# A four-layer graph stack on one core: layer 1's pair rows turned round, its node updates set beside later pairs, the edge checks placed anew

## The chip, the core and the metric

The kernel runs on one core of one Trainium2 chip. It is one launch; the metric is the device time of that launch in microseconds. The core has five engines that run side by side and meet at semaphores: TensorE (PE in the profile; PEld are its weight loads), VectorE (DVE), ScalarE (ACT), GpSimd (POOL) and SyncE (SP), which here only starts transfers. Sixteen DMA engines move data between HBM and the on-chip memory SBUF; matrix products land in PSUM.

## The reference

Four graph layers follow each other on x (4096 nodes, 64 features) with one 4096 x 4096 matrix of edges of 0 and 1. Each layer takes h = relu(layernorm(x)) and adds its result to x. Layer 1 is the one that the change is about; layers 2 and 3 follow it.

```python
h = jnp.maximum(_layernorm(x, axis=-1), 0.0)
x = x + _L0_gnn_ref(h, adj, ...)          # attention of eight heads, then an output attention
# layer 1: c = 1 / r[0] ** 2
h = jnp.maximum(_layernorm(x, axis=-1), 0.0)
x_t = logmap0(h, c)
left, right = x_t @ w_att[:D, 0], x_t @ w_att[D:, 0]
adj_att = jax.nn.sigmoid(left[:, None] + right[None, :] + b_att[0]) * adj
x_local = logmap(h[:, None, :], h[None, :, :], c)          # for every pair of nodes
support_t = jnp.einsum('ij,ijd->id', adj_att, x_local)
x = x + proj(expmap(h, support_t, c), c)                   # node by node: roots, a tanh, divisions
# layer 2
h = jnp.maximum(_layernorm(x, axis=-1), 0.0)
deg = jnp.clip(jnp.sum(adj, axis=1, keepdims=True) + 1.0, 1.0, None)
z = jnp.concatenate([h, (adj @ h + h) / deg], axis=1) @ W + b
out = jax.nn.relu(z)
x = x + out / jnp.maximum(jnp.linalg.norm(out, axis=1, keepdims=True), 1e-12)
# layer 3: weights 0.5 ** (k - rank) for the last 100 edges of a row, by a running count of edges
h = jnp.maximum(_layernorm(x, axis=-1), 0.0)
x = x + w @ (h @ weight) + bias
```

## The kernel before, in words

The 4096 nodes are 32 blocks of 128 (NB = 32), or 8 groups of 512 (NG = 8). Node tiles such as `x` and `h` are 128 x 32 x 64. The program assumes that the edges are exactly 0 or 1 and checks this while it runs: the float matrix is read again in 64 pieces of 128 x 2048 (1 MB each), and `check_rows` (line 960) writes a count of odd values into a column of `bad`. If one is found, or if the inputs are out of range, a slower general program runs at the end. The list `todo` hands out the 64 pieces: `count_odd` (line 964) loads one and checks it, wherever it is called.

Stages, with their places in the profiled execution (microseconds from the start of the span):

**Layer 0**, up to about 1190. It is the larger part of the time, and the change does not touch it.

**The pairs of layer 1**, `pairs_fast`, 1193 to 1648. The distance and score of all node pairs are made group by group. A job is a pair of groups (gi, gj) with gj <= gi, so there are 36 jobs, eight of them on the diagonal. They run row by row with gi rising: (0,0), (1,0), (1,1), (2,0) and so on to (7,7). Jobs are pipelined by hand: while job n is summed (`turn`, `sums`, `last_column`), job n+1 is scored (`score_pair`, `factor`, `weigh`) and job n+2's distances are made (`distance`, `square`). Each job has four slots s = 0 to 3. All instructions of PE, DVE and ACT are issued in the written order (`in_order`); DMAs and GpSimd are not held to it. `bring` moves the sums of a finished job into VT (128 x 4096): line 2408 adds `accj` into the columns of gj, and on the diagonal lines 2406 and 2407 first set the columns of gi. `check_edges` checks one piece in slot 2 of each job and one more in slot 0 beside a diagonal job: 48 of the 64 pieces.

**The ends of layer 1**, `nodes`, built on `finish_steps` (line 2471 on) and `norm_steps`. A quarter is eight blocks (1024 nodes). For each quarter: PE folds VT into node rows (`pvt`, line 2471, evicted by line 2475), then DVE works down a chain of 46 instructions, 16 of them wide (128 x 260 to 128 x 512) and 30 on 128 x 8, with square roots (lines 2500, 2520 and, in the layernorm, 991) and a tanh (line 2503) on ACT. ACT loads another table of functions where root and tanh change places. The result is the new x, the new h, and h as a pair of float16 halves in `HH` (lines 2605 to 2612), which layer 2's matmuls read. The quarters run in rising order after the last pair, in `layers_fast`; at a wait in one quarter up to two steps of the next are put in.

**Layer 2**, `layers_fast`. For eight sets of four blocks (q = 0 to 7) `HH` times the edges (line 2754) and the counts of edges (`dc`, line 2764) are summed for the first half of the nodes; the edges come as bytes, 1 MB for each q (line 2749), in three buffers. Then pairs of groups go through `layer2_group` (first matmul `pz`, line 2680; last DVE step line 2723), while the second half's `segment` sums (lines 2802 and 2811) fill PE. `hT2` is h transposed, made group by group (lines 1008 and 1009).

**Layer 3**, the last loop of `layers_fast`. It has 64 iterations, each with four pairs of `ranks` matmuls (lines 2860 and 2868), `clamp` on DVE and ACT (lines 2884 and 2882), and four `sacc` matmuls of the iteration before (line 2892). Edges come in two transfers of 512 KB for every four iterations (line 2931). Two of every three iterations from the 17th on check half a piece (128 x 1024): 16 pieces in 32 halves; in those iterations three of the four clamps are on ACT. The pieces share two buffers, so a load starts when the piece before the last one is checked. This loop too is in the written order.

On GpSimd and its own queue stand, at the start of `layers_fast`, seven small loads of weights (lines 2566 to 2577), a scaling of one of them (line 2573) and several fills (lines 2579 to 2664).

Of the kernel before, what the change touches and what calls it, by code (L numbers as in the profile page):

```python
# [55 lines left out]
F_C = 1186.920286584489  # L56

HW = N // 2
NS = HW // G
HB = NB // 2  # L60
# [776 lines left out]
def kernel(  # L837
# [76 lines left out]
    bad = npool.tile([P, 2 * NB + 2 + NB // 2], F32, name="bad")  # L914
# [52 lines left out]
    todo = iter(range(2 * NB))  # L967
# [4 lines left out]
    def norm_steps(bs, wide, tag, act=True):  # L972
# [18 lines left out]
        nc.scalar.activation(var, var, AF.Sqrt, bias=eps_t, scale=1.0 / D)  # L991
        yield True
        nc.vector.reciprocal(var, var)
# [1259 lines left out]
    def pairs_fast(es, VT):  # L2253
# [16 lines left out]
        jobs = [(gi, gj) for gi in range(NG) for gj in range(gi + 1)]  # L2270
        edges, sig, far, accs, squares = {}, {}, {}, {}, {}

        with ExitStack() as ss:
# [129 lines left out]
            def bring(gi, gj):  # L2403
                if gi == gj:
                    acci = accs.pop(gi)
                    nc.vector.tensor_copy(VT[0:D, grp(gi)], acci[D : 2 * D])
                    nc.vector.tensor_copy(VT[D : 2 * D, grp(gi)], acci[0:D])
                nc.vector.tensor_tensor(VT[:, grp(gj)], VT[:, grp(gj)], accs.pop("j"), ALU.add)
                del far[gi, gj]
                for way in ways(gi, gj):  # L2410
                    del sig[way], edges[way]

            def check_edges():
                c = next(todo, None)
                if c is not None:
                    count_odd(work, c)
# [5 lines left out]
            with in_order():  # L2422
                for n in range(-2, len(jobs) + 1):
# [3 lines left out]
                    for s in range(4):  # L2427
# [11 lines left out]
                        if later:  # L2439
                            distance(*later, s)  # L2440
                            if s % 2:
                                square(*later, s - 1)
                        if s == 1 and soon:
                            factor(*soon)
                        if n >= 0 and (s == 2 or s == 0 and (not now or now[0] == now[1])):
                            check_edges()
# [5 lines left out]
    def finish_steps(bs, VQ, VT, fold_v, pabs, f, f2, kp, pf, ac2, wide, ps):  # L2452
# [14 lines left out]
        for g in range(bs.start // GB, bs.stop // GB):  # L2467
            pt = ps.tile([P, GB, D1], F32, name="pvt", tag="misc")
# [31 lines left out]
        nc.scalar.activation(un, un, AF.Sqrt)  # L2500
        yield True
        nc.vector.tensor_tensor(arg, un, kp[:, bs], ALU.mult)
        nc.scalar.activation(arg, arg, AF.Tanh)
        nc.vector.reciprocal(un, un)
# [7 lines left out]
        nc.vector.tensor_scalar(one2, xu, p2c, 1.0, ALU.mult, ALU.add)  # L2512
        nc.vector.tensor_tensor(den, ac2[:, bs], uu, ALU.mult)
# [6 lines left out]
        nc.scalar.activation(pp, pp, AF.Sqrt)  # L2520
# [5 lines left out]
        nc.vector.reciprocal(pp, pp)  # L2526
# [12 lines left out]
        yield from norm_steps(bs, wide, "fat")  # L2539
# [5 lines left out]
    def layers_fast(es, wide, *sums):  # L2545
        HO2 = N // 4
        NK = HO2 // G
        cp = es.enter_context(tc.tile_pool(name="lconst", bufs=1))
# [21 lines left out]
        for i, unit in enumerate((1.0 / VALH, 1.0 / (LO * VALH))):  # L2570
# [11 lines left out]
        HH, SS = (  # L2582
            t.rearrange("p (b s d) -> p b s d", s=2, d=D)
            for t in (XA_all.bitcast(F16)[:, 0:N], XA_all.bitcast(F16)[:, N:])
        )
# [10 lines left out]
        ready = []  # L2596

        QB = NB // 4  # L2600

        def nodes(bs):
            yield from finish_steps(bs, *sums, wide, ps)
            hs = wide.tile([P, QB, D], F32, name="hs", tag="fat")
            nc.scalar.activation(HH[:, bs, 0, :], h[:, bs], AF.Copy, scale=VALH)
            yield True
            ready.append(
                nc.vector.scalar_tensor_tensor(
                    hs, h[:, bs], VALH, HH[:, bs, 0, :], ALU.mult, ALU.subtract
                )  # L2610
            )
            nc.scalar.activation(HH[:, bs, 1, :], hs, AF.Copy, scale=LO)


        quarters = [nodes(slice(b, b + QB)) for b in range(0, NB, QB)]
        with in_order():
            for quarter, after in zip(quarters, quarters[1:] + [iter(())]):
                most = 7
                for wait in quarter:
                    for _ in range(min(2, most) if wait else 0):  # L2620
# [41 lines left out]

        hT2 = lp.tile([D + 1, N], F32, name="hT2")
        nc.gpsimd.memset(hT2[D : D + 1, :], 1.0)
        for b0 in range(0, NB, GB):
# [8 lines left out]
        def layer2_group(b0, part, deg):  # L2674
# [48 lines left out]
            nc.vector.tensor_tensor(lo, pu, SS[:, bs, 0, :], ALU.subtract)  # L2723
# [11 lines left out]
        def in_turn_all(*groups):  # L2735
            for pair in zip(groups[::2], groups[1::2]):
                in_turn(*pair)

# [5 lines left out]
        with tc.tile_pool(name="ps_nacc", bufs=6, space=PSUM) as ps_acc:  # L2744
            accs = [ps_acc.tile([P, G], F32, name="nacc", tag="nacc") for _ in range(NS)]
            dc = ps_acc.tile([P, G], F32, name="dc", tag="nacc")
            for q in range(NQ):
# [3 lines left out]
                for t in range(JT):  # L2751
                    j = q * JT + t
                    for k in range(NS):
# [4 lines left out]
                            start=(j == 0),  # L2758
                            stop=(j == NB - 1),
                        )  # L2760
                for t in range(JT):
                    j = q * JT + t
                    for k in range(NS):
# [4 lines left out]
                            start=(j == 0),  # L2768
                            stop=(j == NB - 1),
# [71 lines left out]
            for k in range(0, NS, 2):  # L2841
                in_turn(segment(k), segment(k + 1))
            rank_rows(pl, 1)
# [5 lines left out]
        c = next(todo)  # L2849
        rows = load_rows(work, c)  # L2850
        edges, accs, last, ready = None, {}, None, None
# [72 lines left out]
        with in_order():  # L2924
            for n in range(4 * PAIRS):
# [10 lines left out]
                checks = u and (n - PAIRS) % 3  # L2936
                w = clamp(pvs, checks)
                if checks:
                    if checks == 1:
                        check_rows(rows[:, 0 : HW // 2], c)  # L2940
                    else:
# [101 lines left out]
```

## Time and profile before

| what | value |
|---|---|
| median of three runs | 1974.12 us (1969.64 to 1977.29) |
| profiled execution, time | 1974.73 us |
| its span | 1973.0 us, mean granted TensorE clock 0.943 |
| PE, DVE, ACT, POOL busy over the span | 1773.5, 1596.4, 1424.0, 89.3 us |
| pairs of layer 1 | 1193 to 1648 |
| ends of layer 1 and the first half of layer 2's sums | 1648 to 1743 |
| groups of layer 2 | 1743 to 1812 |
| layer 3 | 1812 to 1966 |

The shares of busy time are means over stages with different limits, so the stages are read one by one. A row of the stage table gives a stretch, its length, then for PE, PEld, DVE, ACT and POOL the busy time and in brackets the count of instructions, then the granted clock of PE (1.00 is full), the busy share of the 16 DMA engines and the GB/s that they moved. In a timeline row the numbers are the start and the duration in us, and the bracket at the end is the idle time of that engine before it and what ended it. In a wait row they are the total, the count and the longest wait.

### The profile page before, as it was taken

The page shows a single profiled execution, that of the slowest core. Times are in us where ns is not written, and L with a number is a line of the kernel's source. Part 1 is how long each engine was busy: PE and PEld are TensorE (multiplying, and loading weights), DVE is VectorE, ACT ScalarE, POOL GpSimd, SP SyncE. Part 2 cuts the span into 40 slices and gives each one's busy share as a digit, 9 for nine tenths or more (in the row PEclk, how much of TensorE's full clock was granted, in tenths as well). Part 3 has the DMA queues.
Part 4 walks back from the last instruction along what each step waited for, and adds up shares of the span by engine and source line. Part 5 has one row for each costly group of instructions (what it writes and reads, how often), then busy time and mean ns, then how long its engine had stood idle before and what let it go on. Part 6 is the DMA issues. An engine that isn't in the chain of part 4 may idle for free. (4 is left out here: it accounts for less than half of the span.)

```text
span 1973.0 us, 44405 instructions
## 1 busy us (share of the span) xinstructions
PE 1773.5 (90%) x19367; PEld 827.7 (42%) x19367; DVE 1596.4 (81%) x2378; ACT 1424.0 (72%) x1461; POOL 89.3 (5%) x127
## 2 busy tenths in 40 slices
PE   5889999999999989998599968999999994899998
PEld 3444444454444445444244442233333332355433
DVE  5769998998779988997768867888887878755676
ACT  2769888899778887995579956777777772333565
POOL 2000100100000000000111100000000001000000
PEclk8889999999999999998699976999999996898999
DMA  8946665325211111102255515543443435342584
GB/s 112 178 127 103 103 102 71 143 107 199 114 50 50 50 50 55 56 2 76 87 182 182 191 34 193 171 144 118 150 144 122 139 103 194 129 128 88 165 276 158
DMA packets 136698, 239.06 MB, mean 121 GB/s; under 512 B 15607, under 2 KB 104999, under 8 KB 122759
## 3 DMA queue, kind: packets, MB, share of 16 engines
q1 hardware_dynamic: 121964, 194.00, 29.4%
q0 software_dynamic: 14528, 42.13, 12.3%
q8 instruction: 153, 2.51, 0.5%
q14 instruction: 53, 0.43, 0.1%
HBM read 245.37 MB, written 49.46 MB: 149 GB/s over the span
## 5 line engine op out<-in xcount | busy, mean ns | idle before, releaser
L1213 ACT ACTIVATE st<-srow,nt 128x2048 int8<-128x2048 f32 x352 | 682.9, 1994 | 90.3 <-DVE B L1219 89.0
L1219 DVE TENSOR_TENSOR B<-st,mres 128x1024 int32<-128x1024 int32 x256 | 311.6, 1220 | 65.1 <-PE accC L1549 39.4
L1549 PE MATMUL accB<-B,ybh 128*32 128x512 fp8e4 x3072 | 256.6, 383 | 18.7 <-DVE B L1219 18.5
L1549 PEld LDWEIGHTS <-ybh 128*32 128x32 bf16 (+1 forms) x6656 | 179.1, 97 | 210.9 <-issue 56.4
L1549 PE MATMUL accC<-B,ycn 128*32 128x512 fp8e4 x2272 | 227.8, 380 | 1.2 <-issue 1.2
L1549 PE MATMUL accC<-mres,ych 128*32 128x512 fp8e4 x2272 | 228.1, 381 | 0.0
L1549 PE MATMUL accD<-B,ybh 128*32 128x512 fp8e4 x2048 | 207.6, 384 | 2.1 <-DVE h L1681 2.1
L1207 DVE TENSOR_SCALAR st<-srow,nt 128x2048 uint8<-128x2048 f32 x160 | 205.3, 1284 | 1.8
L2363 PE MATMUL accj<-sg,who 128*64 128x512 f32 (+1 forms) x512 | 196.7, 614 | 6.4 <-DVE sg L2356 5.9
L2363 PE MATMUL acci<-sg,who 128*64 128x512 f32 (+1 forms) x512 | 196.7, 614 | 0.0
L2319 ACT ACTIVATE yt<-pu,consts 128x512 f32<-128x512 f32 x144 | 98.6, 686 | 97.9 <-PE pu L2318 97.8
L2308 ACT ACTIVATE sg<-pl,rb 128x512 f32<-128x512 f32 x256 | 160.7, 678 | 7.8 <-PE pl L2303 4.7
L1549 PEld LDWEIGHTS <-ych 128*32 128x32 f16 x4096 | 117.6, 97 | 115.3 <-issue 10.2
L1549 PE MATMUL accL<-B,ybh 128*32 128x512 fp8e4 x1536 | 158.0, 387 | 3.6 <-DVE h L1680 3.6
L960 DVE SCALAR_TENSOR_TENSOR raw<-raw 128x2048 f32<-128x2048 f32 (+1 forms) x80 | 148.4, 1856 | 3.3 <-DMA raw<-in_adj_dram 3.3
L1213 ACT ACTIVATE st<-srowo,nto 128x1024 int8<-128x1024 f32 x128 | 138.1, 1138 | 16.3 <-DVE B L1219 13.9
L1227 DVE TENSOR_TENSOR C<-B,mres 128x1024 int32<-128x1024 int32 x114 | 139.5, 1224 | 3.1
L1549 PE MATMUL accC<-C,ych 128*32 128x512 fp8e4 x1824 | 124.0, 383 | 5.3 <-DVE C L1227 5.2
L2882 ACT ACTIVATE w3b<-pv 128x512 int16<-128x512 f32 x160 | 85.3, 596 | 52.9 <-issue 34.3
L2356 DVE SCALAR_TENSOR_TENSOR sg<-pf,sg 128x512 f32<-128x512 f32 x112 | 72.1, 685 | 38.7 <-PE pf L2353 38.7
L2297 PE MATMUL pl<-nm,noid 128*128 128x512 fp8e4 x256 | 82.3, 393 | 13.7 <-ACT sg L2308 13.0
L1549 PEld LDWEIGHTS <-ycn 128*32 128x32 f16 x2272 | 66.1, 98 | 62.1 <-issue 3.2
(515 smaller groups left out, 2738.8 us busy)
## 6 DMA issues: line engine op xcount, KB each, us to landing
raw<-in_adj_dram SPq DMA_DIRECT2D x64, 1024.0 KB, 5.6
mo<-edges SPq DMA_DIRECT2D x32, 512.0 KB, 4.0
noedge<-nmo POOLq DMA_DIRECT2D x32, 512.0 KB, 3.9
nm<-noedge SPq DMA_DIRECT2D x64, 256.0 KB, 3.0
m<-edges SPq DMA_DIRECT2D x32, 512.0 KB, 5.5
srow<-srow_d SPq DMA_DIRECT2D x15, 1024.0 KB, 7.8
mres<-in_adj_dram POOLq DMA_DIRECT2D x8, 1024.0 KB, 36.1
edges<-in_adj_dram POOLq DMA_DIRECT2D x8, 1024.0 KB, 15.0
```

The source lines that it names most:

```text
L960: nc.vector.scalar_tensor_tensor(raw, raw, 0.0, raw, ALU.is_gt, ALU.not_equal, accum_out=bad[:, at : at + 1])
L1207: nc.vector.tensor_scalar(st[:, i, :].bitcast(U8), srow, negs[:, i : i + 1], EDGE, ALU.is_gt, ALU.mult)
L1213: nc.scalar.activation(st[:, i, :], srow, AF.Sign, bias=negs[:, i : i + 1], scale=-1.0)
L1219: nc.vector.tensor_tensor(B.bitcast(I32), st.bitcast(I32), edges.bitcast(I32), ALU.bitwise_and)
L1227: nc.vector.tensor_tensor(C.bitcast(I32), B.bitcast(I32), edges.bitcast(I32), ALU.bitwise_xor)
L1549: ins = nc.tensor.matmul(acc[k * O : (k + 1) * O, :], lhsT=values, rhs=moving(k), start=start, stop=stop,)
L2297: nc.tensor.matmul(pl, lhsT=noid, rhs=nm[:, b, :].bitcast(F8), start=True, stop=False)
L2308: nc.scalar.activation(sg[:, b0 + k, :], pl, AF.Sigmoid, bias=rb[:, j : j + 1], scale=1.0)
L2319: nc.scalar.activation(far[gi, gj][:, b, :], pu, AF.Sigmoid, bias=nb_t, scale=2.0 * DIST_K / (DIST_S * DIST_S),)
L2356: nc.vector.scalar_tensor_tensor(v[:, t, :], pf, F_K3, v[:, t, :], ALU.add, ALU.mult)
L2363: nc.tensor.matmul(acc[r : r + n, :], lhsT=XQ[:, src, cols], rhs=w, start=start, stop=stop)
L2882: nc.scalar.activation(wk, pvs[i, k], AF.Relu)
```

## The change

Five things are changed together.

1. `jobs` runs with gi falling: (7,0) to (7,7), then (6,0) and so on to (0,0). `bring` copies `accj` in row 7 and adds it elsewhere; the diagonal adds both halves of `acci`.
2. When an even row gi = 6, 4, 2 is done, `nodes(gi * GB, ...)` is put into the list `ends`: the quarter of groups gi and gi + 1. `end_nodes` takes one step of it in each of the four slots of a job (up to two near the end). Its PSUM tile comes from the pairs' `pf` pool. What is left after the last job, and the whole of quarter 0, run in `layers_fast` as before, up to three steps of quarter 0 at a wait.
3. In quarters that run beside pairs (`beside`), the three square roots are not ACT's but `inverse_root`: one DVE instruction on the bits, then three Newton rounds of four GpSimd instructions, all on 128 x 8.
4. Layer 2's first sums take q = 7 down to 0, and `hT2` is made from the last group down.
5. Checks: none in `pairs_fast` while `ends` is not empty; `some_checks` in layer 2; 29 pieces instead of 16 in layer 3, so that from the 7th iteration on each one checks half a piece. In the built program 27 pieces are checked beside pairs, 8 in layer 2 and 29 in layer 3.

In the built program quarter 1's last root stands on GpSimd's queue behind the loads and fills at the start of `layers_fast`.

```diff
+QB = NB // 4
+CHECKS_3 = 29
...
+    def inverse_root(name, v, pool):
+        y, t = (pool.tile([P, v.shape[1]], F32, name=n, tag=n) for n in (name, name + "t"))
+        nc.vector.tensor_scalar(
+            y.bitcast(I32), v.bitcast(I32), -0.5, ROOT_BITS, ALU.mult, ALU.add
+        )
+        for _ in range(3):
+            nc.gpsimd.tensor_tensor(t, y, y, ALU.mult)
+            nc.gpsimd.tensor_tensor(t, t, v, ALU.mult)
+            nc.gpsimd.tensor_scalar(t, t, -0.5, 1.5, ALU.mult, ALU.add)
+            nc.gpsimd.tensor_tensor(y, y, t, ALU.mult)
+        return y
...
-        nc.scalar.activation(var, var, AF.Sqrt, bias=eps_t, scale=1.0 / D)
-        yield True
-        nc.vector.reciprocal(var, var)
+        if beside:
+            nc.gpsimd.tensor_scalar(var, var, 1.0 / D, LN_EPS, ALU.mult, ALU.add)
+            yield True
+            var = inverse_root("ln_root", var, wide)
+            yield True
+        else:
...
-        jobs = [(gi, gj) for gi in range(NG) for gj in range(gi + 1)]
+        jobs = [(gi, gj) for gi in reversed(range(NG)) for gj in range(gi + 1)]
+        ends = []
...
+                accj = accs.pop("j")
+                if gi == NG - 1:
+                    nc.vector.tensor_copy(VT[:, grp(gj)], accj)
+                else:
+                    nc.vector.tensor_tensor(VT[:, grp(gj)], VT[:, grp(gj)], accj, ALU.add)
                 if gi == gj:
                     acci = accs.pop(gi)
-                    nc.vector.tensor_copy(VT[0:D, grp(gi)], acci[D : 2 * D])
-                    nc.vector.tensor_copy(VT[D : 2 * D, grp(gi)], acci[0:D])
-                nc.vector.tensor_tensor(VT[:, grp(gj)], VT[:, grp(gj)], accs.pop("j"), ALU.add)
+                    for to, r in ((0, D), (D, 0)):
+                        half = VT[to : to + D, grp(gi)]
+                        nc.vector.tensor_tensor(half, half, acci[r : r + D], ALU.add)
+                    if gi % 2 == 0 and gi:
+                        ends.append(nodes(gi * GB, lambda: ps_f.tile([P, G], F32, name="pf", tag="pf")))
...
+            def end_nodes(most):
+                while ends and most:
+                    wait = next(ends[0], None)
+                    if wait is None:
+                        ends.pop(0)
+                    most = 0 if wait else most - 1
...
+                        busy = bool(ends)
+                        if now:
+                            end_nodes(1 if later else 2)
                         if s == 1 and soon:
                             factor(*soon)
-                        if n >= 0 and (s == 2 or s == 0 and (not now or now[0] == now[1])):
+                        if n >= 0 and not busy and (s == 2 or s == 0 and (not now or now[0] == now[1])):
                             check_edges()
...
+        if beside:
+            yield False
+            norm, un = un, inverse_root("un_root", un, wide)
+            nc.gpsimd.tensor_tensor(norm, norm, un, ALU.mult)
+            nc.gpsimd.tensor_tensor(arg, norm, kp[:, bs], ALU.mult)
+            yield True
+            nc.scalar.activation(arg, arg, AF.Tanh)
...
-        nc.scalar.activation(pp, pp, AF.Sqrt)
+        if beside:
+            yield False
+            pp = inverse_root("pp_root", pp, wide)
...
-            for quarter, after in zip(quarters, quarters[1:] + [iter(())]):
-                most = 7
+            for quarter, after in zip(ends, ends[1:] + [iter(())]):
+                most = 12
                 for wait in quarter:
-                    for _ in range(min(2, most) if wait else 0):
+                    for _ in range(min(3, most) if wait else 0):
...
-        for b0 in range(0, NB, GB):
+        for b0 in reversed(range(0, NB, GB)):
...
+        def some_checks(left):
+            n = len(todo) - CHECKS_3
+            with tc.issue_after(valued[-1].ins):
+                for _ in range(-(-n // left)):
+                    count_odd(work, todo.pop(0))
...
-            for q in range(NQ):
+            for n, q in enumerate(reversed(range(NQ))):
...
-                checks = u and (n - PAIRS) % 3
+                checks = n >= 4 * PAIRS - 2 * CHECKS_3
```

`valued` holds the last DVE step of each layer 2 group, so that the checks there are issued after it.

## The prediction

> **What bounds the kernel now.** I read the stage table first, then PE's waits between the stages, then the timelines of DVE and GpSimd in that gap, last the loads of layer 3.
>
> ```profile
> 1193.00:1648.00 455.00, 431.08 (x2283) 147.13 (x2282) 371.89 (x401) 332.80 (x470) 0.00 (x0) 0.97 0.44 146
> 1648.00:1743.00 95.00, 65.60 (x388) 34.49 (x389) 71.47 (x217) 30.66 (x52) 10.66 (x15) 0.75 0.44 149
> 1743.00:1812.00 69.00, 64.68 (x450) 42.48 (x448) 33.80 (x101) 19.99 (x52) 7.02 (x10) 0.90 0.42 122
> 1812.00:1966.00 154.00, 150.41 (x860) 62.24 (x859) 113.25 (x202) 92.81 (x180) 1.82 (x3) 1.00 0.58 195
> ```
> PE bounds the pairs (431 of 455 us) and layer 3 (150 of 154) and nearly layer 2's groups. In the 95 us between, it is busy 65.6 us at a clock of 0.75, so the work there is about 49 us at full clock: 46 us are for the taking.
>
> Who PE waited for in that stretch:
> ```profile
> PE nacc L2754 <- ACT XAf L2612: 18.8, 3, 15.1
> PE pvt L2471 <- DVE who L2475: 9.4, 2, 5.6
> ```
> and rows of the timeline of DVE, the last of PE:
> ```profile
> 1643.69 2.29 DVE L960 SCALAR_TENSOR_TENSOR raw<-raw 128x2048 f32<-128x2048 f32 x1 [0.24 <-DMA raw<-in_adj_dram]
> ...
> 1674.59 0.69 DVE L2608 SCALAR_TENSOR_TENSOR hs<-h,XAf 128x512 f32<-128x512 f32 x1 [0.69 <-ACT XAf L2605]
> ...
> 1725.58 0.69 DVE L2608 SCALAR_TENSOR_TENSOR hs<-h,XAf 128x512 f32<-128x512 f32 x1 [0.69 <-ACT XAf L2605]
> ...
> 1743.28 0.39 PE L2680 MATMUL pz<-w2f,hT 65*128 65x128 f32 x2
> ```
> PE waits there for the quarters' ends: the first is done at 1674.6, the fourth at 1725.6, 17 us apart, and layer 2's groups start 17.7 us after the fourth. DVE carries the chain, and the last checks (2.3 us each) stand in front of it.
>
> The pairs: VT's additions, PE's longest waits, and the GpSimd row nearest to the new work (from the groups by form).
> ```profile
> L2408 DVE TENSOR_TENSOR VT<-VT,accj x36: 676/689/690, 1219.6 to 1647.8; 128x512 f32<-128x512 f32 x36
> PE pl L2297 <- ACT sg L2308: 13.0, 27, 1.2
> PE accj L2363 <- DVE sg L2356: 5.9, 7, 2.2
> L2725 POOL TENSOR_TENSOR x<-x,b3f 128x256 f32<-128x256 f32 x8 | 6.0, 754 | 51.6 <-DVE h L981 50.4 <-DVE ln_var L993 1.2
> ```
> GpSimd's timeline after the pairs:
> ```profile
> 1654.74 0.20 POOL L2565 MEMSET w2f<- 1x128 f32 x1 [463.41 <-DVE fing L2484]
> 1672.15 0.85 POOL L2573 TENSOR_SCALAR w2e<-w2e 64x64 f32<-64x64 f32 x2 [12.20 <-issue]
> 1674.11 3.50 POOL L2664 MEMSET hT<- 1x4096 f32 x1
> ```
> Layer 3: two stretches of the stage table, and the landing of the tile raw:
> ```profile
> 1875.00:1900.00 25.00, 25.00 (x148) 10.51 (x146) 19.05 (x32) 15.78 (x30) 0.00 (x0) 1.00 0.82 276
> 1937.50:1941.50 4.00, 4.00 (x24) 1.48 (x23) 2.80 (x6) 2.34 (x5) 0.00 (x0) 1.00 1.03 395
> DMA to landing us min/median/max: 5.0/5.3/6.3
> ```
> 35 intervals of VT in 428 us make 12.2 us a job, 3.1 us a slot. GpSimd needs 23 us from 1654.7 to 1677.6, half of it until the weights land. In layer 3 PE is full while the DMA engines are at 0.82; the last row is a checked piece's time from issue to landing there.
>
> **The change part by part** (against the profiled 1974.7 us, 0.6 above the median of the runs).
>
> *Beside pairs, counts.* Checks go from 48 to 27: 21 x 2.36 us = 50 us of DVE leave. Three quarters come in; one, added up from the timeline, is 46 DVE instructions and 15.7 us, so 47 us. DVE's load is unchanged, but its place is not: checks stood only in slot 2 (and 0 by the diagonal), steps stand in all four. Slots 1 and 3 hold 2.35 us of factor or weigh; with the heaviest step (2.0 us) they take 4.3 of 3.1. I give 1 us for each of about five such slots that PE's two-deep buffers don't cover: +5. If DVE has slack enough, 0; if every step shows, 15.
>
> *Order of rows.* The same 36 jobs; only start and end differ. The row before began with light diagonal jobs at 12 us each and ran out with two cheap ones (10.2 and 7.2 us). Now heavy jobs stand first and light ones last: +3. Two diagonals (5 and 3) lose their checks: -3.
>
> *Newton on GpSimd.* Each beside quarter has 38 GpSimd steps plus one scaling, in chains of 12 to 14. No row shows such an operation on 8 columns. The nearest row is 0.754 us for 256 columns (L2725). Flat, a chain is 9 to 10.6 us, which rival 2 works out. The Trainium skill (GPSIMD Engine Reference, section 3.1 Elementwise) gives 0.156 us of dispatch and 2.6 cycles an element: 0.71 us for the 256, near the row, and by my estimate 0.18 us for 8, a chain of 2.2 to 2.5 us. I take 0.2, a chain of 2.4 to 2.8, because the rule hits the row that it can be held to. A second rule speaks against the change: the skill (SBUF — State Buffer, section Who interferes with whom) says that a VectorE instruction with two SBUF inputs and a GpSimd one that reads SBUF exclude each other, and the second blocks fully. factor, weigh and half the steps are such. No row here shows it. With it a chain may take a whole job, but while DVE, held in the written order, waits for the root, GpSimd runs free, so a wait is at most about 2.5 us. Mostly a slot lies between root and use; 1 us each for six chains is in the +5 above.
>
> *End of the pairs.* Quarter 1 starts at (2,2), with three jobs left. Its chains stand in short jobs: behind VT of (1,0) comes the wait for tanh's argument, then weigh of (0,0); behind VT of (1,1) the root of pp, four wide and about ten small instructions, and only then VT of (0,0). By their durations 12.5 and 11 us, against 10.2 and 7.2: +6. Sum for the pairs: 5 + 3 - 3 + 6 = +11 (0 to +20).
>
> *The gap.* Quarter 0 alone is left, with quarter 1's tail between its steps. From its VT: VT 2.0, pvt and who 1.8, down to V 3.9, Square and uu 2.0, root, two table loads and tanh 2.0, small ones 2.9, root 0.4, factors 1.6 with quarter 1's h, four wide and quarter 1's hs 3.5, layernorm 4.4: 25 us to hs. Added wait: in DVE's written order quarter 1's last root stands in the middle of quarter 0, and on GpSimd it is behind w2f, the DMA issues, the wait for the weights and the fills. Those took 23 us; started 7 us before VT of (0,0), they end at +16, DVE is there at +8. Transfers ahead are 4 MB instead of 5, so I take 5 us (0 to 10). hs at +30. PE has meanwhile done q = 7 to 3 (5 x 4.7 us from +3, a little cold: +29), then it waits in its order for wsq (4.5 us behind hs), then transposes 5.2, q = 2 to 0 13.2, and 5 up to pz with filling: pz at +58. Before, VT of the last job began at 1646.0 and pz at 1743.3: +97. Gain 39 (29 to 47). But 29 nacc and 13 dc of the second half filled that gap, now 17: 3 us come later. **-36.**
>
> *Layer 2.* 8 checks x 2.36 = 19 us of DVE, 33.8 of 69 busy. Two stand behind each pair of groups, one inside a chain; they push the next group's zt by some 3 to 5 us, and three pairs follow. PE has nacc work to fill with, 65 of 69. On SP's queue three piece loads stand before the masks of a later segment and wait for a buffer, that is for the checks. I take +6 (0 to 15).
>
> *Layer 3.* 13 more pieces, all in checked iterations of 2.16 us. DVE: clamp 0.69 + check 1.30 = 1.99; ACT 1.57; PE 2.16 hides them. DMA: 1 MB of piece and 0.5 MB of edges per two iterations, 1.57 MB in 4.32 us = 364 GB/s; before, 276. The skill (DMA: Bandwidth & Descriptors, section Where 436 GB/s comes from) puts the HBM limit of a core at about 358; that would be 4.39 us, 2 us over 29 pieces. The last row of the table has 395 in 4 us: the trace allows more for short. The nearer limit is the buffers: a load is issued when a second half is checked (3.46 us after its first half began) and is wanted 8.64 - 3.46 = 5.2 us later; it took 5.3 in the median, 6.3 beside edges. Two pieces take 3.4 + L: 8.7 to 9.7 against 8.64, times 14.5: +1 to +15. I take +7.
>
> Sum: +11 - 36 + 6 + 7 = -12 on the profile; **1962** by the median.
>
> **The rivals.**
> 1. *Loads bind layer 3 (slower).* Place: the check waits for its piece, clamps behind it on DVE, PE behind them. For: window of 5.2 us, latency 5.3, DMA share to go from 0.82 to 1.07 by proportion. Against: 395 GB/s was reached. It decides when L passes 7.5 us: (3.4 + 7.5 - 8.64) x 14.5 = 33, and the sum is +14: 1988.
> 2. *Newton chains hold DVE (slower).* At 0.754 an operation a chain is 9 to 10.6; minus one or two slots, 16 us a quarter in three waits, 48 in all, minus some 2 us of slack a job: about +30 in place of the 11: 1981 to 1990. Against: the skill's per-element rule.
> 3. *Paid back.* The gap closes by 29 only (GpSimd's queue late by 10), layer 2 +10, layer 3 +10: 1974 +- 6. For: the middle values are all inside my bounds.
> 4. *Better than summed.* Pairs +3, layer 2 and 3 +2 each, gap 40: 1941.
> That the change doesn't do what it says: quarter 1 only partly lies beside pairs; this is in the sum.
>
> **How the numbers follow.** My forecast 0.35 with 1952 to 1968, rival 4 0.20, rival 3 0.20, rivals 1 and 2 0.12 and 0.13. Half a percent, 10 us, is about what a measurement of this kernel can tell. Faster by more: 0.20 + 0.30 of my own case = 0.50. Same: 0.05 of mine, 0.15 of rival 3 = 0.20. Slower: the rest, 0.30. The range 1938 to 1990 takes in rival 4 and most of 1 and 2; my own case alone is 1952 to 1968.
>
> **What would show it.** VT of (0,0) about 10 us after 1646; pz some 58 us behind it; on GpSimd 8-column operations near 0.2 us; DVE's ln_root waiting for GpSimd about 5 us; zt of the second pair of groups behind two checks; in layer 3 PE above 95% and pieces landing in under 6.5 us. Wrong if GpSimd's operations are 0.5 us and more, if PE waits for w3b in layer 3, or if pz comes later than 70 us behind VT.

## The result and the profile after

The changed kernel takes 1980.64 us in the median of ten runs (1977.05 to 1987.19), the kernel before 1974.80 on the same chip (1969.06 to 1978.12): a ratio of 1.0035, with a 95% interval of 1.0019 to 1.0050. It is slower by about 6 us. The forecast was 1962.

To see where the time went, both traces were cut at the same four events: the start of the last `bring` (VT of job (0,0), or in the kernel before its first half, (7,7)), the first `pz` of layer 2, the first `w3b` and the last `sacc` of layer 3. Between them (us):

| stretch | before | after | moved | forecast |
|---|---|---|---|---|
| start of the last `bring` (from the start of the span) | 1646.0 | 1671.9 | +25.9 | +11 |
| from there to `pz` (the gap) | 97.1 | 53.1 | -44.0 | -36 |
| `pz` to the first `w3b` (layer 2) | 70.7 | 79.8 | +9.1 | +6 |
| `w3b` to the last `sacc` (layer 3) | 148.4 | 163.5 | +15.1 | +7 |
| sum | | | +6.1 | -12 |

Each length is from one trace. The code up to the first VT is the same in the changed kernel and in the ten kernels with the descending order that follow; the first VT stands at 1221.7 in the changed kernel (1219.6 in the kernel before) and between 1217.6 and 1223.6 in the ten. So in a time counted from the start of the span some 3 us either way mean nothing.

The same four stretches in the stage table of the changed kernel (columns as in the table of before):

```profile
1221.70:1671.90 450.20, 413.20 (x2212) 144.04 (x2211) 349.71 (x475) 314.72 (x451) 34.57 (x111) 0.96 0.27 87
1671.90:1725.00 53.10, 50.61 (x332) 24.18 (x333) 28.16 (x80) 14.71 (x25) 10.18 (x22) 0.92 0.70 239
1725.00:1804.80 79.80, 70.92 (x483) 45.65 (x482) 51.61 (x122) 20.57 (x54) 7.06 (x10) 0.89 0.68 214
1804.80:1968.30 163.50, 155.01 (x819) 60.83 (x833) 123.39 (x219) 104.21 (x203) 1.45 (x2) 0.98 0.77 262
```

In the first row PE is idle 37 us of 450, where it was idle 24 of 455 in the pairs before. The second is the gap, and it did what it should: PE is busy 50.6 of 53.1 us. In the last, PE is idle 8.5 us.

**The pairs.** Two places carry the loss. One is the first job behind a finished quarter: the interval from VT to VT is 18.0 us for (5,0) and for (3,0), where (6,0), (4,0) and (2,0) have 13.7. DVE's timeline there, then PE's waits in the last jobs by PE's own view, and DVE and GpSimd in those jobs:

```profile
1396.33 0.69 DVE L2431 TENSOR_TENSOR VT<-VT,accj 128x512 f32<-128x512 f32 x1 [2.60 <-PE acci L2386]
1397.12 1.39 DVE L2436 TENSOR_TENSOR VT<-VT,acci 64x512 f32<-64x512 f32 x2
1398.54 1.29 DVE L2379 SCALAR_TENSOR_TENSOR sg<-pf,sg 128x512 f32<-128x512 f32 x2
1400.43 0.43 DVE L2515 TENSOR_TENSOR who<-pf,pabs 128x260 f32<-128x260 f32 x1 [0.60 <-PE pf L2511]
1406.07 0.43 DVE L2515 TENSOR_TENSOR who<-pf,pabs 128x260 f32<-128x260 f32 x1 [5.22 <-PE pf L2511]
1406.42 1.22 DVE L2360 SCALAR_TENSOR_TENSOR yt<-sqy,yt 128x1024 f32<-128x1024 f32 x1
```
```profile
PE accj L2386 <- DVE VT L2431: 10.6, 1, 10.6
```
```profile
1650.72 2.36 DVE L2360 SCALAR_TENSOR_TENSOR yt<-sqy,yt 128x1024 f32<-128x1024 f32 x2
1650.89 1.10 POOL L982 TENSOR_TENSOR un_roott<-un_root 128x8 f32<-128x8 f32 x1 [40.99 <-DVE un_root L978]
1652.07 1.06 POOL L983 TENSOR_TENSOR un_roott<-un_roott,un 128x8 f32<-128x8 f32 x1
1653.22 0.20 POOL L984 TENSOR_SCALAR un_roott<-un_roott 128x8 f32<-128x8 f32 x1
1653.50 0.20 POOL L985 TENSOR_TENSOR un_root<-un_root,un_roott 128x8 f32<-128x8 f32 x1
...
1656.31 0.20 POOL L2544 TENSOR_TENSOR arg<-un,kp 128x8 f32<-128x8 f32 x1
1656.79 0.23 DVE L2555 SCALAR_TENSOR_TENSOR arg<-un_root,rabs,arg 128x8 f32<-128x8 f32 x1 [3.71 <-ACT arg L2546]
...
1658.82 2.35 DVE L2367 SCALAR_TENSOR_TENSOR sg<-yt,sg 128x1024 f32<-128x1024 f32 x2
1661.09 0.68 DVE L2431 TENSOR_TENSOR VT<-VT,accj 128x512 f32<-128x512 f32 x1
```

In the first fence `who` waits 5.22 us for a `pvt` that stands behind PE's sums, and `factor` (L2360, tile yt) is queued behind `who`. But `factor` works for the job after, and PE does not wait for it here. PE's rows in the same job, then two stretches of the stage table, and last the one wait of PE in that job in the kernel with the descending order alone (section 5):

```profile
1399.28 1.11 PE L2511 MATMUL pf<-fold_v,VT 128*128 128x65 f32 x8 [1.55 <-DVE sg L2379]
1401.99 1.06 PE L2386 MATMUL accj<-sg,who 128*64 128x512 f32 x1
1405.03 1.00 PE L2511 MATMUL pf<-fold_v,VT 128*128 128x65 f32 x8
```
```profile
1397.60:1401.00 3.40, 1.85 (x13) 1.14 (x12) 2.61 (x5) 0.69 (x1) 0.00 (x0) 1.00 0.02 7
1401.00:1404.40 3.40, 3.40 (x10) 0.77 (x8) 0.00 (x0) 1.26 (x2) 0.00 (x0) 0.50 0.26 77
```
```profile
1399.04 0.64 PE L2363 MATMUL accj<-sg,who 128*64 128x512 f32 x1 [0.79 <-DVE sg L2356]
```

PE waits once, 1.55 us instead of 0.79, at the first `pvt`, for DVE's sg behind VT. Then its clock is at 0.50 for 3.4 us, which costs half of that, 1.7. And the two `pvt` (lines 2471 before, 2511 here) are PE's own work, some 0.84 us each. That is 0.8 + 1.7 + 1.7 = 4.2 of the 4.3 us.

At the end of the pairs, in the rows of DVE and GpSimd from 1650 on, DVE waits 3.7 us for the chain and the tanh, then takes twelve small instructions and `weigh` (L2367), and only then VT of (1,1) at 1661.1. For all of that PE stands for 10.6 us. The clock follows:

```profile
1650.00:1655.00 5.00, 1.20 (x10) 0.16 (x8) 2.97 (x6) 0.63 (x2) 3.46 (x9) 0.86 0.00 0
1655.00:1660.00 5.00, 0.00 (x0) 0.00 (x0) 2.94 (x14) 0.21 (x1) 1.10 (x6) 0.50 0.00 0
1660.00:1670.00 10.00, 6.33 (x16) 1.39 (x16) 6.55 (x16) 0.00 (x0) 3.73 (x15) 0.64 0.09 14
1670.00:1680.00 10.00, 5.92 (x22) 4.36 (x23) 6.57 (x15) 0.63 (x1) 6.17 (x12) 0.53 1.01 355
1685.00:1690.00 5.00, 5.00 (x35) 2.02 (x34) 3.50 (x22) 3.42 (x5) 1.17 (x6) 1.00 0.92 370
```

PE's next 64-column sums run at 1.06 to 1.11 us where the same ones at full clock take 0.59.

**The gap.** The rows that answer to hs, pz and GpSimd's queue, from the timelines of DVE, PE and GpSimd:

```profile
1698.39 0.69 DVE L3041 SCALAR_TENSOR_TENSOR hs<-h,XAf 128x512 f32<-128x512 f32 x1 [0.70 <-ACT XAf L3038]
...
1725.20 0.39 PE L2715 MATMUL pz<-w2f,hT 65*128 65x128 f32 x2
```
```profile
1668.39 0.20 POOL L2622 MEMSET w2f<- 1x128 f32 x1 [1.49 <-PE acci L2386]
...
1679.16 3.50 POOL L2699 MEMSET hT<- 1x4096 f32 x1
1682.76 0.20 POOL L1008 TENSOR_SCALAR ln_var<-ln_var 128x8 f32<-128x8 f32 x1
```

The last hs comes 26.5 us behind VT. GpSimd passes its queue in 14.4 us, 1668.4 to 1682.8, where the same queue took 23 before.

**Layer 3.** The stage table in its middle, and the transfers of raw (DVE's wait for them, and the time to landing):

```profile
1875.00:1900.00 25.00, 22.82 (x129) 9.67 (x129) 19.15 (x34) 15.67 (x31) 0.00 (x0) 1.00 0.93 321
```
```profile
  DMA raw<-in_adj_dram: 25.1, 25
...
DMA to landing us min/median/max: 4.8/6.9/8.2
```

A piece lands in 6.9 us in the median, not 5.3, and DVE waits 25 times, 25.1 us in all. PE has fallen from 25.0 of 25 us to 22.8.

### The profile page after: what moved, and what is told of

The parts are those of the page before. It is cut to its first block, busy times and chain, and to the rows that moved or that the text cites. A ratio compares the mean times of both kernels' runs of the same rounds, so it can differ in the third digit from the quotient of the medians.

```text
span 1978.3 us, 44491 instructions
## 1 busy us (share of the span) xinstructions
PE 1782.1 (90%) x19352; PEld 825.1 (42%) x19367; DVE 1579.5 (80%) x2375; ACT 1425.2 (72%) x1472; POOL 123.4 (6%) x244
## 5 line engine op out<-in xcount | busy, mean ns | idle before, releaser
L2386 PE MATMUL accj<-sg,who 128*64 128x512 f32 (+1 forms) x512 | 199.9, 621 | 15.3 <-DVE VT L2431 10.6
L963 DVE SCALAR_TENSOR_TENSOR raw<-raw 128x1024 f32<-128x1024 f32 (+1 forms) x93 | 150.3, 1620 | 25.4 <-DMA raw<-in_adj_dram 25.4
L2927 ACT ACTIVATE w3b<-pv 128x512 int16<-128x512 f32 x186 | 98.2, 598 | 55.8 <-issue 31.9
L2379 DVE SCALAR_TENSOR_TENSOR sg<-pf,sg 128x512 f32<-128x512 f32 x112 | 72.2, 686 | 28.9 <-PE pf L2376 26.6
```

The lines of the kernel that those rows point to most:

```text
L963: nc.vector.scalar_tensor_tensor(raw, raw, 0.0, raw, ALU.is_gt, ALU.not_equal, accum_out=bad[:, at : at + 1])
L2379: nc.vector.scalar_tensor_tensor(v[:, t, :], pf, F_K3, v[:, t, :], ALU.add, ALU.mult)
L2386: nc.tensor.matmul(acc[r : r + n, :], lhsT=XQ[:, src, cols], rhs=w, start=start, stop=stop)
L2927: nc.scalar.activation(wk, pvs[i, k], AF.Relu)
```

## The experiments

Kernels that ran together were compared with runs of the kernel before on the same chip; the ratios below are to those. Stretches are cut as above; "pairs" is from the first `accj` brought into VT to the last (450.3 us in the changed kernel, 428.2 before).

### 1. pvt in the odd slots

```diff
-        ends = []
+        ends, fresh = [], [0]
...
+                        fresh[0] = 0
                         ends.append(nodes(gi * GB, ...))
...
-                        if now:
+                        if now and (fresh[0] > 1 or s % 2):
+                            fresh[0] += 1
                             end_nodes(1 if later else 2)
```


> The changed kernel, except that the first two steps of a quarter's end (the two groups of pvt) are taken in slots 1 and 3 only. Theory A (PE, in its written order, stands at pvt in slot 0 until VectorE has read the first turned bank and written VT, and the clock falls after the stop): jobs (5,0) and (3,0) go from 18.0 us to about 13.7, as (6,0), (4,0) and (2,0) are, and (2,2) to (1,0) loses about 1 us: 8 to 10 us less, about 1971. Rival B (these two jobs are long because VectorE has the steps on top of its work, wherever they stand): both stay at 17 us or more, and the time within 3 us of the changed kernel.

Measured: 1983.45 us, ratio 1.0049 (1.0024 to 1.0074). Jobs (5,0) and (3,0) take 16.2 us, and the pairs 445.1, 5.2 us less; between A's 13.7 and B's 17. The mechanism is A's all the same: in (5,0) PE waits 0.8 us and its clock is at 1.00 throughout. Taken together with the job behind it, (5,0) lasts 28.3 us instead of 31.1; with the descending order alone it is 26.6, and the 1.8 between are, but for 0.1, the two `pvt`, which PE has to do wherever they stand. But layer 2 grew from 79.8 to 87.7 us:

```profile
1720.30:1808.00 87.70, 79.10 (x483) 51.56 (x482) 53.52 (x123) 19.66 (x52) 7.06 (x10) 0.80 0.63 203
```

One check more falls to it (9 instead of 8, and 26 instead of 27 beside pairs: 2.3 us of DVE); otherwise the instructions are nearly the same, while the granted clock is 0.80 instead of 0.89. So what one stage gains a later one may lose by the clock. These are single traces: how much of the 8 us the moved steps cause was not tried.

### 2. Quarter 1 behind the pairs again

```diff
-        ends = []
+        ends, late_q = [], []
...
-                    if gi % 2 == 0 and gi:
+                    if gi == 2:
+                        late_q.append(gi)
+                    elif gi % 2 == 0 and gi:
...
-                        busy = bool(ends)
+                        busy = bool(ends or late_q)
...
-        ends.append(nodes(0, ...))
+        for b in (QB, 0):
+            ends.append(nodes(b, ...))
```


> The changed kernel, with quarter 1 taken out of the pairs and put back behind them ahead of quarter 0, with ScalarE's roots. No checks take its place beside the pairs. Theory A (the end of the last jobs is paid for by the root's chains, but the gap's 17 us a quarter is worth more): the last three jobs go from 41.3 us to about 31, the gap from 53 us to 68 or 70, together 5 to 7 us slower than the changed kernel, about 1987. Rival B (PE has enough sums of layer 2 to hide a second quarter): the gap grows by under 8 us, and the kernel is 2 to 5 us faster than the changed one, about 1977.

Measured: 1973.66 us, ratio 0.9995 (0.9979 to 1.0011). The last three jobs take 23.1 us in place of 41.3, the gap 60.2 in place of 53.1: B, and by more. Quarter 1 beside pairs costs 18.2 us and saves 7.1. Behind the pairs it is woven between the steps of quarter 0 (the two hs are 6.5 us apart), and PE has layer 2's sums to do meanwhile: it is busy 51.7 of the 60.2 us.

### 3. Layer 3's pieces in halves, and with fewer loads

```diff
+    def load_half(pool, c, o):
+        raw = pool.tile([P, HW // 2], F32, name="rawh", tag="rawh", bufs=4)
+        at = c // NB * HW + o * (HW // 2)
+        nc.sync.dma_start(raw, adjT[c % NB * P : (c % NB + 1) * P, at : at + HW // 2])
+        return raw
...
-                    count_odd(work, todo.pop(0))
+                    c = todo.pop(0)
+                    for o in range(2):
+                        at = ...
+                        check_rows(load_half(work, c, o), at)
...
-                        rows = load_rows(work, c)
+                        rows = [load_half(work, c, o) for o in range(2)]
```


> The changed kernel, with layer 2's and layer 3's pieces of the adjacency loaded as two halves into four half buffers, so that a half is loaded again as soon as it is checked. The same bytes in the same time. Theory A (the buffer's window binds: a piece is asked for when its second half is checked, 5.2 us before it is wanted, and lands in 6.7): the window becomes 7.3 us, VectorE's wait for raw falls from 25 us to under 8, layer 3 from 163.5 us to 150 to 154, in all about 10 us less, 1970. Rival B (the rate of the transfers binds, at 316 to 325 GB/s): layer 3 stays above 160, within 3 us of the changed kernel.

The other kernel loads only some of the pieces again:

```diff
                         c = todo.pop(0)
-                        rows = load_rows(work, c)
+                        if len(todo) * 15 % 28 < 15:
+                            rows = load_rows(work, c)
```


> The changed kernel, with 13 of layer 3's 28 later loads of adjacency pieces left out: the check is made on what the buffer holds, so VectorE's and ScalarE's work is the same and 13 MB of transfers are gone. Theory A (loads make layer 3 long): layer 3 from 163.5 us to 149 to 153, in all 10 to 14 us less, about 1968. Rival B (the 26 more checked iterations make it long on VectorE): layer 3 stays above 160 us.

Measured: halves 1965.49 us, ratio 0.9959 (0.9943 to 0.9975), layer 3 153.6 us; fewer loads 1970.15 us, 0.9990 (0.9974 to 1.0006), layer 3 152.7 us. With halves layer 2, whose pieces are halves too, took 76.0 us instead of 79.8. The middle of layer 3, first with halves, then with fewer loads:

```profile
1875.00:1900.00 25.00, 24.84 (x144) 10.55 (x146) 21.10 (x36) 17.61 (x34) 0.00 (x0) 1.00 1.00 353
1900.00:1925.00 25.00, 24.90 (x145) 10.54 (x145) 21.25 (x35) 17.60 (x34) 0.00 (x0) 1.00 0.99 357
```
```profile
1875.00:1900.00 25.00, 24.89 (x146) 10.66 (x148) 21.11 (x37) 17.31 (x34) 0.00 (x0) 1.00 0.81 266
```

Both bring PE back to 24.9 of 25 us here with the same checks on DVE, so in this stretch the checks are not the cause, and transfers are. With halves the same bytes flow at 353 to 357 GB/s instead of 316 to 321: the rate was not the limit, the time from a buffer's release to its use was. That is A in both. No wait for rawh is left in layer 3. From the 16th iteration to the last (by the first clamp of each) the loop takes 118.9 us in the changed kernel and 108.9 in both of these, as in the kernel before: the loads cost 10.0 us.

The checks do cost something, elsewhere. Layer 3 stays 4 to 5 us above the 148.4 of the kernel before. The nine iterations 7 to 15, which that kernel did not check, in the kernel before and in the one with halves:

```profile
1833.20:1852.60 19.40, 19.40 (x109) 7.21 (x108) 11.55 (x19) 9.73 (x19) 0.00 (x0) 1.00 0.33 108
```
```profile
1819.70:1843.30 23.60, 22.66 (x108) 7.22 (x109) 16.49 (x29) 14.19 (x28) 0.00 (x0) 1.00 0.79 270
```

They last 2.62 us each instead of 2.16, in the changed kernel and in both of these, with no wait for a piece in the one with halves: 4.2 us. The rows and the code say why, though no kernel tried it. Until the 16th iteration the four tiles `pv` are all in the four buffers of one pool; later the fourth has a buffer of another. With a check, three clamps run one behind the other on ACT (1.57 us), and the last of the next iteration's four first matmuls starts at 1828.7, when the third clamp has ended:

```profile
1827.11 1.57 ACT L2937 ACTIVATE w3b<-pv 128x512 int16<-128x512 f32 x3 [1.05 <-issue]
1828.26 0.85 PE L2915 MATMUL pv<-late_x,LDf 32*128 32x512 bf16 x2
```

From the 17th iteration on the same pair takes 0.39 us instead of 0.85. The remaining 0.9 us of the 15.1 stand in the first seven iterations, where the clock is 0.71 over 10 us instead of 1.00.

### 4. Both edits together

The edit of section 2 and the halves of section 3, with no further change.

> Both edits that helped by themselves: quarter 1 behind the pairs, and the pieces of layer 2 and 3 as halves in four half buffers. Theory A (two separate places, so the gains add up: 7 us and 15 us of 1980): about 1959, layer 3 at 152 to 156, pairs 432, gap 60. Rival B (layer 2's granted clock differs with every shift of the work before it and takes back a part): layer 2 at 80 us or more, 1964 to 1968.

Measured: 1958.19 us, ratio 0.9919 (0.9889 to 0.9950): faster than both kernels. Pairs 430.5, gap 61.5, layer 3 153.8 as expected; layer 2 in the profiled run 84.1, B's mark. The median is A's, the profiled run (1963.92) B's. Six runs lie between 1953.84 and 1965.53, the shortest with a mean clock of 0.956 and the longest with 0.943.

### 5. The descending order alone

```diff
-        jobs = [(gi, gj) for gi in range(NG) for gj in range(gi + 1)]
+        jobs = [(gi, gj) for gi in reversed(range(NG)) for gj in range(gi + 1)]
```
and the changed `bring` without `ends`, in the kernel before.

> The kernel before with the descending order of rows alone: VT is copied in the first row and added to later, all quarters behind the pairs, checks as before (48 beside pairs, 16 pieces in layer 3). Theory A (the order costs little: the same 36 jobs, with heavy ones in front and light ones last): from the first VT to the last 428 to 433 us, where before has 428.2, in all 1973 to 1980. Rival B (the order itself makes the long jobs (5,0) and (3,0) and the long end): these two stay at 17 us or more, and the pairs take over 440.

Measured: 1973.63 us, ratio 1.0008 (0.9987 to 1.0028). Pairs 425.6 us, with (5,0) and (3,0) at 13.71 each: A. The last `bring` starts at 1647.0, 1.0 us later than before. From here the changed kernel's pairs can be split: 397.3 us up to (2,2) and 28.3 for the last three jobs with the order alone, 408.9 and 41.3 with the quarters. That is 11.6 us for the steps beside full jobs, net of the checks that left, and 13.0 for the end.

### 6. Newton on VectorE

```diff
-            nc.gpsimd.tensor_tensor(t, y, y, ALU.mult)
+            nc.vector.tensor_tensor(t, y, y, ALU.mult)
```
and so for all steps of the roots.

> The changed kernel with the same Newton steps on VectorE in place of GpSimd. Theory A (in the last jobs VectorE waits for GpSimd's chain, whose first two operations take 1.1 us each beside VectorE's, and PE waits for VT behind it): a chain of 12 to 14 takes VectorE 2.4 to 2.8 us in place of a wait of 3.2 to 5.9, jobs (1,0) to (0,0) go from 41.3 us to 36 to 39; in the other jobs beside quarters it costs up to 2 us for each of four to six chains: 1975 to 1983. Rival B (GpSimd's chains lie hidden, and the last jobs are long by the number of small steps): the last three jobs take 41 us or more.

Measured: 1985.01 us, ratio 1.0058 (1.0043 to 1.0074). The last three jobs take 39.6 us, just outside A's 36 to 39 and below B's 41. The pairs are 4.7 us shorter and the gap 5.0 longer. So where the roots run decides 1.7 us of the 18 that quarter 1 costs at the end: the chain of twelve then takes DVE 2.4 us of its own, and PE's long wait shrinks from 10.6 to 9.7. The rest stays with the steps' place in DVE's queue. GpSimd is no worse a place for the roots than DVE.

### 7. The first two steps behind factor and weigh

```diff
-        ends = []
+        ends, fresh = [], [0]
...
+                        fresh[0] = 0
                         ends.append(nodes(gi * GB, ...))
...
+                        fresh[0] += 1
+                        first = fresh[0] <= 4
-                        if now:
+                        if now and not first:
                             end_nodes(1 if later else 2)
...
                         if s == 3 and soon:
                             weigh(*soon)
...
+                        if now and first and s % 2:
+                            end_nodes(1)
```


> The changed kernel, with the first two steps of a quarter's end (pvt on PE, who on VectorE) taken at the end of slots 1 and 3, behind factor and weigh in VectorE's order; one check more falls to layer 2. Theory A (in the two long jobs VectorE waits 5.2 us at who for pvt, which stands behind PE's sums, while factor, which PE's next weights hang on, is queued behind who): (5,0) and (3,0) go from 18.0 us to 13.7 to 14.5, as without quarters, about 8 us less in all. Rival B (VectorE has too much work in these jobs): they stay above 16 us, as when the steps were only put into the odd slots.

Measured: 1974.78 us, ratio 1.0009 (0.9991 to 1.0028). (5,0) and (3,0) take 15.4 us, and the pairs 442.9, 7.4 us less. DVE's timeline in (5,0):

```profile
1398.39 2.35 DVE L2360 SCALAR_TENSOR_TENSOR yt<-sqy,yt 128x1024 f32<-128x1024 f32 x2
1401.29 0.43 DVE L2520 TENSOR_TENSOR who<-pf,pabs 128x260 f32<-128x260 f32 x1 [0.55 <-PE pf L2516]
```

`factor` runs while PE does its sums and `pvt`, and the wait of 5.22 us has become 0.55. But that wait was not what the jobs lost: section 1 left `factor` behind `who` and gained as much, for (5,0) with (5,1) lasts 28.2 us here and 28.3 there. Here too PE waits 0.8 us and is at full clock, and the 1.7 us over the order alone are again the two `pvt` of 0.84 us. So of A's 4.3 us 2.6 came, and not by A's mechanism. Of the 7.4 us, 4.2 come from the last three jobs (37.1 in place of 41.3); up to (2,2) it is 3.0, so other jobs gave back 2.2 of the 5.2 that the two gained.

### 8. Layer 2's checks cut short

```diff
-                    count_odd(work, todo.pop(0))
+                    c = todo.pop(0)
+                    raw = work.tile([P, 64], F32, name="raws", tag="raws")
+                    nc.sync.dma_start(raw, adjT[0:P, 0:64])
+                    check_rows(raw, c)
```


> The changed kernel with the 8 checks of layer 2 and their loads cut from 2048 columns to 64 (the rest of those pieces isn't checked): 8 times 2.3 us of VectorE and 8 MB leave. Theory A (the checks stand between the groups' chains on VectorE): from the first pz to the first w3b 73 to 76 us in place of 79.8. Rival B (layer 2 is longer because more sums and counts are left for it, and PE's clock falls in it): 78 us or more.

Measured: 1975.46 us, ratio 1.0010 (0.9998 to 1.0022). Layer 2 takes 73.4 us: A, 6.4 of the 9.1 by these two traces. The kernel of section 3 with fewer loads has the changed kernel's layer 2 unchanged, and there it took 77.0 us at a clock of 0.90, below B's mark too; so the checks with their loads are worth 3.6 to 6.4 us. A kernel without them altogether has no time on record. Rows of the changed kernel show how: the check stands between two steps of a group's chain.

```profile
1747.75 0.75 DVE L2734 TENSOR_REDUCE nrm<-sq 128x4 f32<-128x256 f32 x2 [0.79 <-ACT sq L2731]
1748.82 2.29 DVE L963 SCALAR_TENSOR_TENSOR raw<-raw 128x2048 f32<-128x2048 f32 x1 [0.32 <-DMA raw<-in_adj_dram]
1751.04 0.08 DVE L963 DVE_READ_ACCUMULATOR raw<-raw 128x1 f32 x1
1751.04 0.23 DVE L2735 TENSOR_SCALAR nrm<-nrm 128x4 f32<-128x4 f32 x2
```

Layer 3 was 165.9 us instead of 163.5 in the same trace. In the kernels of sections 1, 2 and 7 it was 166.0, 165.6 and 168.5. Each has the two buffers and a wait for raw of 25 to 27 us. From the 16th iteration on they take 119.9 to 121.6 us instead of 118.9; why stays open.

### 9. Three edits together

The edits of section 4 with that of section 7.

> Three edits together: quarter 1 behind the pairs, half buffers for layers 2 and 3, and the first two steps of a quarter's end behind factor and weigh in slots 1 and 3 (layer 2 has 9 checks). If theory A of the late steps holds: 7 to 8 us less than the first two alone, pairs at 423 to 425, in all about 1950. If rival B holds: pairs at 428 to 432, 1956 to 1960.

Measured: 1956.27 us, ratio 0.9922 (0.9894 to 0.9950). Pairs are at 428.9, B's figure; against section 4, with 0.9919, there is no difference that these runs can tell. Where quarter 1 is already gone from the end, the late steps are worth 1.6 us of the pairs.

## Why the prediction failed, by its own steps

**End of the pairs (+6): the step that failed most.** It measured +13.0 against the order alone and 18.2 against the same kernel without quarter 1 there. The mechanism was named rightly (DVE behind VT of (1,0) waits for the tanh, then `weigh`; the root of pp and the small steps stand ahead of VT of (0,0)). The sizes were wrong in three ways. Job (1,0), which takes 15.7 us instead of 12.1, was not counted: 3.7. The base was the end of the rising order, 10.2 and 7.2, while these light jobs take 9.6 and 6.6 with the order alone, 1.2 less in sum, and 5.5 and 5.5 without the quarter and checks. And (1,1) took 14.8, not 12.5 (with (0,0) at 10.8 for 11): there was no price for PE's clock, which is at 0.50 to 0.64 in the 25 us from 1655. With this the pairs came to +25.9, past the bounds of 0 to +20. The Trainium skill (TensorE: Matmul & The Clock Gate, Part 1, The HAM clock gate) says that an idle window of about 3.4 us halves the clock, and that a busy window of that length brings it back. Here the trace agrees: 10.6 us of waiting, 0.50, full again by 1685. In job (5,0) it differs from the page: 3.4 us in which PE was busy for 1.85, with one wait of 1.55, were followed by 3.4 us at 0.50. By these figures a shorter pause halves the clock too.

**Beside pairs (+5, from 0 to 15).** 11.6 us for the jobs up to (2,2), inside the bounds but double the value. 8.5 us stand in two jobs, 18.0 against 13.7 each. The heavy step on DVE in a slot of 3.1 us was priced. PE's own part was put at nothing: two `pvt` of 0.84 us for each quarter in a stage that PE bounds, and the 3.4 us at half clock behind the wait at the first of them.

**Order of rows (+3 - 3).** The sum came out: +1.0 at the last `bring` with the order alone, which keeps all checks. The -3 did not show: (5,5) and (3,3) take 23.0 us together with the order alone and 23.0 in the changed kernel, where they have no checks.

**Newton (0.2 an operation).** Right in the main. Free, an operation takes 0.20 us every 0.28, so a chain of 12 is 3.4 us against my 2.4 to 2.8. From 8 columns at 0.20 to 256 at 0.754 it is 2.2 ns for a column, which the skill's 2.6 cycles (GPSIMD Engine Reference, section 3.1 Elementwise) fit at its 1.2 GHz. The other 0.18 us, by my estimate from these two rows, do not grow with the columns; no row before showed them, so that 0.2 was hit is in part luck. The skill's second rule holds too: beside `factor`, with its two SBUF inputs, the first two took 1.10 and 1.06 until it ended. That costs such a chain about 1.7 us, and rival 2's flat price is refuted.

**The gap (-36): -44.0.** The chain of 25 us to hs was right, measured 26.5 with the wait. The added wait for GpSimd's queue was 0.93 us, not 5, since that queue took 14.4 us instead of 23. From hs to pz it took 26.6 us, near the 28 of my sum. The bounds, 29 to 47 less 3, just hold the gain. But its split was read wrongly: quarter 1's own share is 7.1 us, not a third of the gap, because two quarters can be woven.

**Layer 2 (+6): +9.1,** inside 0 to 15; the checks are 3.6 to 6.4 of it (section 8). The rest fits the more sums and counts left for it, 483 PE instructions against 460, but was not tried.

**Layer 3 (+7, from +1 to +15): +15.1.** The formula for DVE's wait was right and its input was not. With L = 6.9 instead of 5.3 to 6.3, the excess over 8.64 is 1.66 us, times 14.5 makes 24; DVE waited 25.1. Two steps failed. Not all of that wait reaches PE: the loads cost 10.0 us (section 3). And the checks were taken to be hidden behind PE's 2.16 us; in nine iterations they are not, and take 4.2 us. With 0.9 at the start that is 15.1, so the bound of +15 was met by two errors of opposite sign. Why a piece lands later than before is open: with fewer loads it was 7.0 us in the median at 250 to 266 GB/s, while it was 5.3 before at 276, so the traffic alone does not say. DVE waiting for a piece, clamps behind it and PE behind them is rival 1's mechanism, below its mark of 7.5 us. The other half of the argument, the rate of 364 GB/s asked against the skill's about 358, cost little: with halves the kernel ran at up to 357 with PE at 24.9 of 25.

The errors add up: +15 pairs, -8 gap, +3 layer 2, +8 layer 3 make 18, the way from -12 to +6. The change was paid back, as in rival 3, though not by the sizes it gave: the gap closed by more than forecast, and pairs and layer 3 gave it back.

## What to carry to other kernels

Work put beside a stage that PE fills costs at least PE's own part of it, and any pause that it puts into PE may cost clock on top (3.4 us at 0.50 behind a wait of 1.55). The last, light jobs are the worst place, because there a chain on one engine idles PE outright. Before moving a chain off the path, ask how much of it could be woven with its neighbour where it stands: here two quarters behind the pairs cost 7 us more than one. And when loads double, do not count on the landing time of the trace of before (5.3 us there, 6.9 here), and buy window by smaller buffers released sooner: half buffers gave 10 us for no bytes and no memory.

## What was not expected of the hardware

- The same program differs by its clock. Six runs of the kernel of section 4 had mean clocks of 0.956 to 0.943 and took 1953.84 to 1965.53 us. Layer 2 took 70.7 us at 0.90 in the kernel before and, with the same code, 67.2 at 0.95 in that of section 5. The skill (TensorE: Matmul & The Clock Gate, Part 1) says that the activity window runs freely, so a shift of the work ahead moves which pauses fill it; the rows agree with that but do not prove it.
- A GpSimd operation on 8 columns took 0.20 us alone and 1.10 beside a VectorE instruction with two SBUF inputs.
- Reads beside PE at 99% went at up to 357 GB/s over 25 us, and at 316 to 321 with the same bytes in whole pieces, asked for later.
